# Three instead of two last channel groups taken image by image, with three x tiles loaded one step ahead and three spare buffers for pieces, in a convolution and whitening kernel

## The chip, the core and the metric

The kernel runs on one core of one Trainium2 chip. The metric is the device time of one execution in microseconds (us), the median of several runs. A profile is one execution of the same program, recorded by the hardware profiler; its times are counted from the first recorded instruction. The engines are named as in the profile: PE is the matrix engine (TensorE), PEld its weight loads, DVE the vector engine, ACT the scalar engine, POOL GpSimd, and SP the engine that does nothing here but issue DMAs. Each engine works through its own list of instructions in order.

## The reference: what is computed

The input `x` has 4 images of 64 channels of 256 x 256 float32. Two layers follow each other.

```python
# layer 0: a causal 2-D convolution per channel, with a filter that is an outer product
hx = filter_X(z) * decay          # 256 taps for each of the 64 channels
hy = filter_Y(z) * decay
k  = einsum('ijk,imk->ijmk', hx, hy)
y  = irfft2(rfft2(x) * rfft2(k) / fft_size)[:256, :256] + x * bias
# layer 1: whitening over the 64 channels
x1   = y as (64, 4*256*256)
x1_s = x1[:, ::9]                 # every ninth pixel
cov  = x1_s @ x1_s.T / n + 0.01 * I
out  = isqrt_newton_schulz(cov, 5) @ (x1 - mean(x1_s))
```

Because the 2-D filter is an outer product, layer 0 is two 1-D convolutions, one along each axis of the image, and each of them is a product with a 256 x 256 Toeplitz matrix (each row is the row above, shifted by one tap).

## The kernel before

**Tiling.** The 64 channels are 8 groups of 8 (`CG`). A step is one channel group `g` of one image `n`, so there are 32 steps; `steps` (lines 107 and 108) is their order. The first six groups run group by group, with the four images inside; the last two groups run image by image: (6,0), (7,0), (6,1), (7,1) and so on. The x data of a step is one tile of 128 partitions x 16 KB, of which the pool `xpool` has four. A step has four items of two channels, `c` = 0, 2, 4, 6. This text numbers the items 0 to 127 in their order: item `j` is step `j // 4`, channels `2 * (j % 4)` and the next.

**Matrix work.** An item is multiplied twice by Toeplitz blocks (`f` = 0 in its first stage, `f` = 1 in its second). The function `group` (line 394) computes at once the first stage of one item and the second stage of the item two places before it; this text calls the call for item `j` group `j`. So item `j` has its first stage in group `j` and its second in group `j + 2`. Only the first two items and the last two are computed alone (`half_group`). In a group, 80 recorded matmuls of line 220 alternate between the two items: the first matmul is of the first-stage item, the second of the second-stage item, and so on. Even groups take the four 64-row blocks of the matrix in the order 0, 1, 2, 3 and odd ones in the reverse; in an even group the second matmul reads the upper half (partitions 64 to 127) of the second-stage matrix. After the matmuls ACT copies the first-stage result (line 409), DVE adds bias and x to the second-stage result in place in the x tile (line 412), and `store` (line 420) sends the two channels to `y_d` in DRAM by two DMAs of 256 KB on SP's queue (line 425). `pack` then lets DVE copy sampled pixels to `samp` (line 319), at a pace of some 2.9 us for each group.

**SP's list.** All loads of the loop stand in SP's list, in program order, behind the stores of the same group (lines 587 to 596): first one 512 KB part of x (two channels), then, where the dictionary `blocks` says so, one part of a Toeplitz block (line 193, 192 or 256 KB), then, where the dictionary `early` says so, one 2 MB piece of `y_d` (line 357). As the stores wait for DVE's line 412 of their group, everything of a group's slot in SP's list is issued after that group's matmuls have ended. The DMAs use eight semaphores in turn, and an issue waits until the DMA eight places before it has landed.

**Toeplitz blocks.** `toep[g]` holds both matrices of the 8 channels of a group in 16 KB of each partition; the pool `tpool` has three buffers. A block comes in eight parts: part 0 to 3 is `f` = 0 and 4 to 7 is `f` = 1; in each `f` the first two parts are the lower half of the partitions and the last two the upper half; of each two, the first is channels 0 to 3 and the second channels 4 to 7. The dictionary `blocks` (lines 371 to 376) maps the number of a group to the part that is issued in its slot. In the kernel before, block 6 is issued in the slots of groups 82 to 89 and first used in group 96; block 7 is issued in the slots of groups 90 to 97, its part 6 in that of group 96, and item 100 is the first item of channel group 7, whose second stage is in group 102.

**The end.** When all channels of an image are stored, its 8 pieces of 2 MB can be read back. `homes` names the 13 buffers in which pieces are held, in turn: two of the pool `epool`, three of `tpool`, four of the samples and four of x tiles. Nine pieces are loaded inside the loop (`early`), four more after it, and piece `i + 13` when piece `i` has been written out. `covariance(n)` (line 333, 116 matmuls) takes the samples of one image; it stands on PE in front of a group for images 0 to 2, and after the loop for image 3. `whitening` then makes the 64 x 64 matrix `W` on PE, DVE and ACT, and from there each piece is multiplied by `W` (line 635), evacuated by ACT and DVE (lines 639, 640) and written out (line 645).

Of the kernel before, what the change touches and what calls it, by code (L numbers as in the profile page):

```python
# [38 lines left out]
F32 = mybir.dt.float32  # L39
# [6 lines left out]
NB, C, L = 4, 64, 256  # L46
P, H2 = 128, 2
EMB, ORDER = 33, 64
PIX = L * L
CG = 8  # L50
# [4 lines left out]
EPS = 0.01  # L55
N_ITER = 5
GW = P + L
FP = 4096

TURN = 6.283185  # L60
# [4 lines left out]
def conv_whiten_kernel(ctx: ExitStack, tc: tile.TileContext, a: dict, out: bass.AP):  # L65
    nc = tc.nc
    x = a["x"]

    const = ctx.enter_context(tc.tile_pool(name="const", bufs=1))
    xpool = ctx.enter_context(tc.tile_pool(name="xpool", bufs=4))  # L70
    epool = ctx.enter_context(tc.tile_pool(name="epool", bufs=2))
    spool = ctx.enter_context(tc.tile_pool(name="spool", bufs=NB))
    tpool = ctx.enter_context(tc.tile_pool(name="tpool", bufs=3))
    o1pool = ctx.enter_context(tc.tile_pool(name="o1pool", bufs=4))
# [3 lines left out]
    y_d = [dram.tile([H2 * C, PIX // H2], F32, tag=f"y{n}", name=f"y_d{n}") for n in range(NB)]  # L78
    g_d = dram.tile([P, GW], F32, tag="g", name="g_d")
    g0_d = dram.tile([2 * CG, GW], F32, tag="g0", name="g0_d")  # L80

# [18 lines left out]
    def load_x(t, g, n, c):  # L100
        nc.sync.dma_start(
            out=t[:, c : c + 2],
            in_=x[n, g][:, c : c + 2],
        )


    steps = [(g, n) for g in range(C // CG - 2) for n in range(NB)]
    steps += [(g, n) for n in range(NB) for g in range(C // CG - 2, C // CG)]

    x_tiles = [xpool.tile([P, CG, H2, L], F32, tag="in", name=f"x{u}") for u in range(4)]  # L110
    for c in range(0, CG, 2):
        load_x(x_tiles[0], *steps[0], c)
        if c == 0:
            nc.sync.dma_start(out=decay, in_=a["decay"])
    nc.sync.dma_start(out=mask, in_=a["mask"])
# [5 lines left out]
    for n in range(NB):  # L121
        t = spool.tile([P, FP], F32, tag="samp", name=f"samp{n}")
        samp.append(
# [14 lines left out]

    taps = scratch[:, 11:13, :].rearrange("p a w -> p (a w)")[:, 0:GW]
    nc.gpsimd.memset(taps[:, L:GW], 0.0)  # L140

# [13 lines left out]
    for i in range(3):  # L155
        for u in range(2):
# [3 lines left out]
            arg, k, nxt = (scratch[:, 2 + 3 * i + v, half] for v in range(3))  # L160
# [22 lines left out]
    def new_toeplitz(g):  # L183


        return tpool.tile([P, 2, CG, L], F32, tag="toep", name=f"toep_{g}")

    def load_toeplitz(t, g, f, half, lo=0, hi=CG, issue=nc.sync):
        source, row = (g0_d, f * CG + lo) if g == 0 else (g_d, f * C + g * CG + lo)


        skip = 0 if f == half else HP
        issue.dma_start(
            out=t[half * HP : (half + 1) * HP, f, lo:hi, skip:],
            in_=bass.AP(
                tensor=source.tensor,
                offset=source.offset + row * GW + skip,
                ap=[[1, HP], [GW, hi - lo], [1, L - skip]],
            ),
        )  # L200
# [126 lines left out]
    def covariance(n):  # L327

        pc = psA.tile([P, C + 1], F32, tag="psA", name=f"pc{n}")
        for b in range(H2):  # L330
            for j in range(NJ):
                half = slice(C * (j % 2), C * (j % 2 + 1))
                nc.tensor.matmul(  # L333
                    pc[half],
                    lhsT=samp[n][:, b, j, 0:C],
                    rhs=samp[n][:, b, j, :],
                    start=(b == 0 and j < 2),
                    stop=(b == H2 - 1 and j >= NJ - 2),
                    skip_group_check=True,
                )  # L340
        nc.vector.scalar_tensor_tensor(cov, pc, 1.0 / NSAMP, cov, ALU.mult, ALU.add)


    pieces = [(n, q) for n in range(NB) for q in range(PIX // H2 // FP)]


    homes = [
        {"t": (tpool, "toep"), "s": (spool, "samp"), "i": (xpool, "in"), "e": (epool, "extra")}[k]
        for k in "eetssiistitis"
    ]  # L350

    def load_y(i):

        n, q = pieces[i]
        pool, tag = homes[i % len(homes)]
        t = pool.tile([P, FP], F32, tag=tag, name=f"yi_{n}_{q}")
        nc.sync.dma_start(out=t, in_=y_d[n][:, q * FP : (q + 1) * FP])  # L357
        return t
# [10 lines left out]


    blocks = {}
    for g in range(1, C // CG):
        first = 16 * g - 14 if g < C // CG - 1 else 16 * g - 22
        for part in range(8):
            k = first + (part * 12 // 8 if g < C // CG - 2 else part)
            blocks[k // 4, k % 4 * 2] = (g, part)

    early = {
        (26, 4): 1, (27, 0): 1, (27, 4): 1, (28, 0): 1, (29, 2): 1, (30, 0): 1, (31, 0): 1, (31, 2): 1, (31, 4): 1
    }  # L380
    orders = [list(range(L // HP)), list(reversed(range(L // HP)))]

# [11 lines left out]
    def group(first, second):  # L394

        units = []
        g1, n1, c1, x1, o1s1 = first
        g2, n2, c2, x2, o1s2 = second
        for u in range(2):
            job2 = (bank(f"p2_{g2}_{n2}_{c2 + u}"), o1s2[u], toep[g2][:, 1, c2 + u, :])  # L400
            job1 = (bank(f"p1_{g1}_{n1}_{c1 + u}"), x1[:, c1 + u], toep[g1][:, 0, c1 + u, :])
            units.append((job1, job2))

        toeplitz_products(units, orders[0])
        orders.reverse()
        for u in range(2):
            o1 = o1pool.tile([P, H2, L], F32, tag="o1", name=f"o1_{g1}_{n1}_{c1 + u}")
            for to, fr in ((slice(0, HP), slice(HP, P)), (slice(HP, P), slice(0, HP))):
                nc.scalar.copy(o1[to], units[u][0][0][fr])  # L409
            o1s1.append(o1)  # L410
            ch = g2 * CG + c2 + u
            nc.vector.scalar_tensor_tensor(  # L412
                x2[:, c2 + u], x2[:, c2 + u], bias[:, ch : ch + 1], units[u][1][0],
                ALU.mult, ALU.add,
            )

        store(second)
        pack(2.92)
# [138 lines left out]
    with tc.manual_schedule(  # L557
        engines={engines.PE, engines.SP, engines.DVE, engines.Activation, engines.Pool}
    ):
        toep = {0: new_toeplitz(0)}  # L560

        for f, lo, hi in ((0, 0, 2), (0, 2, 4), (0, 4, 6), (1, 0, 2), (0, 6, 8), (1, 2, 4), (1, 4, 8)):
            for half in range(2):
                load_toeplitz(toep[0], 0, f, half, lo, hi, nc.scalar if half else nc.sync)
        for c in range(0, CG, 2):
            load_x(x_tiles[1], *steps[1], c)
        for i, (g, n) in enumerate(steps):
            xt = x_tiles[i % 4]
            for c in range(0, CG, 2):
                item = (g, n, c, xt, [])  # L570
                if g == C // CG - 1 and n > 0 and c == 2:
                    covariance(n - 1)
                if len(pending) == 2:
                    group(item, pending.pop(0))
                else:
                    half_group(item, 0)
                pending.append(item)
                if i == 0 and c == 6:

                    fold = const.tile([P, C], F32, tag="fold", name="fold")  # L580
                    nc.vector.tensor_tensor(fold, ident[:, 0:C], ident[:, C:P], ALU.add)

                    nc.scalar.activation(bf[:, 0:1], samp[0][:, 0, 0, C : C + 1], AF.Sqrt)
                if i == 1 and c < CG - 2:
                    load_pick(c // 2 * 3, c // 2 * 3 + 3)

                if i + 2 < len(steps):
                    load_x(x_tiles[(i + 2) % 4], *steps[i + 2], c)
                if (i, c) in blocks:
                    tg, part = blocks[i, c]  # L590
                    if part == 0:
                        toep[tg] = new_toeplitz(tg)
                    lo = part % 2 * CG // 2
                    load_toeplitz(toep[tg], tg, part // 4, part // 2 % 2, lo, lo + CG // 2)
                for _ in range(early.get((i, c), 0)):
                    load_next()
        g, n, c, yt, _ = pending[0]
        for item in pending:
            half_group(item, 1)
            pack(1.0)  # L600
            store(item)

        pack()
        i15 = place(2 * C, rows=C).rearrange("p (u c) -> p u c", u=2)
        for u in range(2):
            nc.gpsimd.tensor_scalar(i15[:, u], ident[0:C, 0:C], 1.5, None, ALU.mult)  # L606
        ones = place(P, rows=C)
        nc.gpsimd.memset(ones, 1.0)
        for lo in range(CG // 2, CG, 2):
            pack_by_pe(g, n, yt, slice(lo, lo + 2))  # L610
        spin(4)
        covariance(NB - 1)
        while len(loaded) < len(homes):
            load_next()
        W, shift = whitening(i15, ones)
# [3 lines left out]
    for i, (n, q) in enumerate(pieces):  # L619
# [5 lines left out]
        part = 512 if i == 0 else 1024 if i == 1 or i > len(pieces) - 3 else 2048  # L625
        for w in range(FP // 1024):

# [78 lines left out]
```

## Time and profile before

| What | Value |
|---|---|
| median of 3 runs | 903.03 us (901.62 to 903.9) |
| span of the profiled execution | 902.1 us |
| PE busy | 781.2 us, 87% of the span |
| DVE busy | 581.5 us, 64% |
| ACT busy | 395.5 us, 44% |
| DMA | 285.61 MB, mean 317 GB/s |
| matmuls of line 220 | 10,080 records, 64% of the chain that ended last |
| reads of pieces (line 357) | 32 x 2 MB, median 15.6 us to landing |
| parts of Toeplitz blocks (line 193) | 63 on SP's queue, 3.0 / 5.8 / 7.5 us to landing (least, median, most) |

The profile page has a row of digits for each engine: the span in 40 equal slices of 22.55 us, each digit the busy share of a slice in tenths. PEclk is the granted clock of PE in tenths of full speed. The chain that ended last is followed back from the last instruction, at each step to what released it. An issue of a DMA is shown on SP's queue ("SPq") with the time at which it was issued; "to landing" is the time from there until its semaphore shows the data in place. For about every second DMA the record has no landing of its own.

### The profile page before, as it was taken

To read this page: it belongs to the slowest core of one execution; us is meant where nothing else is said; L and a number is where in the kernel's file an instruction comes from. 1 tells how busy PE (TensorE), PEld (TensorE's weight loads), DVE (VectorE), ACT (ScalarE), POOL (GpSimd) and SP (SyncE) were. 2 spreads that over 40 slices of the span, in tenths; PEclk is the share of its full clock that TensorE was granted. 3 is DMA by queue.
4 is the path that set the end of the run, shared out by engine and by line. 5 is a ranking of instruction groups with operands and counts; after the bars stand their busy time and mean duration, and the time that the engine had idled before them with its cause. 6 is when DMAs were issued, how large, how long until landed. Compare 5 with 4: busy or idle time off the path is not lost.

```text
span 902.1 us, 28046 instructions
## 1 busy us (share of the span) xinstructions
PE 781.2 (87%) x11928; PEld 647.5 (72%) x11928; DVE 581.5 (64%) x801; ACT 395.5 (44%) x676; POOL 14.5 (2%) x40
## 2 busy tenths in 40 slices
PE   8999999999999999999999999999999565666200
PEld 7999999999999999999999999999533111212000
DVE  3487778877888778877888877877688332233200
ACT  2655554545455555545454444442487232233200
POOL 1000000000000000000000000000010000000000
PEclk9999999999999999999999999999999766866755
DMA  7988889798788888888997899979999999999998
GB/s 209 327 262 252 242 261 271 234 273 251 247 263 261 244 264 259 258 250 267 293 275 241 285 351 356 335 237 390 375 401 429 430 432 432 429 434 430 430 430 355
DMA packets 117912, 285.61 MB, mean 317 GB/s; under 512 B 8891, under 2 KB 91116, under 8 KB 110108
## 3 DMA queue, kind: packets, MB, share of 16 engines
q1 hardware_dynamic: 113436, 244.94, 79.0%
q0 software_dynamic: 3056, 37.95, 10.0%
q8 instruction: 95, 1.56, 0.7%
q10 hardware_dynamic: 1296, 0.93, 0.4%
q14 instruction: 29, 0.24, 0.1%
HBM read 149.35 MB, written 134.44 MB: 315 GB/s over the span
## 4 chain that ended last, share of the span: by engine, by line
PE 74%; DMA 11%; another core or an unknown queue 7%; DVE 0%; issue 0%; SPq 0%; ACT 0%; POOLq 0%; DVEq 0%
PE p L220 64%; DMA out_dram<-yi 5%; DMA yi<-y_d 5%; PE po L635 4%; PE pc L333 2%; PE ph L252 1%; PE pk L300 1%; PE spin L442 1%; DMA toep<-g_d 0%; PE busy L152 0%; PE pm L158 0%; SPq L357 0%; DMA scratch<-in_zw_dram 0%; DVE yi L640 0%
## 5 line engine op out<-in xcount | busy, mean ns | idle before, releaser
L220 PE MATMUL p<-toep,x 64*64 64x64 f32 (+3 forms) x5040 | 579.5, 284 | 0.8 <-issue 0.8
L220 PE MATMUL p<-toep,o 64*64 64x64 f32 (+3 forms) x5040 | 579.5, 284 | 0.0
L220 PEld LDWEIGHTS p<-toep,x 64*128 64x128 f32 (+1 forms) x5040 | 535.7, 166 | 24.4 <-issue 1.3
L220 PEld LDWEIGHTS p<-toep,o 64*128 64x128 f32 (+1 forms) x5040 | 536.7, 166 | 10.7 <-issue 0.2
L409 ACT COPY o<-p 64x512 f32<-64x512 f32 x504 | 292.8, 581 | 294.2 <-PE p L220 286.6
L319 DVE COPY_PREDICATED samp<-mask,x 128x464 f32<-128x464 int32 (+3 forms) x351 | 297.2, 847 | 9.8 <-DVE x L412 0.2
L412 DVE SCALAR_TENSOR_TENSOR x<-x,bias,p 128x512 f32<-128x512 f32 x252 | 179.8, 744 | 121.3 <-PE p L220 117.3
L635 PE MATMUL po<-yi,chain 64*64 64x512 f32 x1024 | 143.7, 720 | 60.4 <-DMA yi<-y_d 60.4
L640 DVE TENSOR_SCALAR yi<-po,shift 128x512 f32<-128x512 f32 x128 | 96.1, 751 | 109.0 <-PE po L635 100.7
L635 PEld LDWEIGHTS po<-yi,chain 64*64 64x64 f32 x1024 | 48.0, 162 | 155.2 <-issue 150.5
L639 ACT ACTIVATE yi<-po,shift 128x512 f32<-128x512 f32 x128 | 88.0, 687 | 116.7 <-PE po L635 116.0
L333 PE MATMUL pc<-samp 128*64 128x65 f32 x464 | 14.9, 223 | 0.0
L333 PEld LDWEIGHTS pc<-samp 128*64 128x64 f32 x464 | 14.3, 137 | 0.3
L645 POOL DMA_DIRECT2D out_dram<-yi x19 | 10.5, 554 | 130.5 <-DMA out_dram<-yi 55.1
L606 POOL TENSOR_SCALAR chain<-ident 64x64 f32<-64x64 f32 x2 | 1.0, 519 | 606.6 <-PE ph L252 606.6
L286 DVE COPY o<-ph 64x256 f32<-64x256 f32 x8 | 3.4, 422 | 9.7 <-PE ph L252 9.6
L152 PE MATMUL busy<-idle 128*128 128x128 f32 x64 | 9.4, 307 | 0.0
L152 PEld LDWEIGHTS busy<-idle 128*128 128x128 f32 x64 | 8.9, 222 | 0.2 <-issue 0.2
L300 PE MATMUL pk<-x,pick 128*128 128x56 f32 (+1 forms) x72 | 8.3, 292 | 0.0
L300 PEld LDWEIGHTS pk<-x,pick 128*128 128x128 f32 x72 | 8.1, 192 | 0.1
L442 PE MATMUL spin<-ident 128*128 128x128 f32 x50 | 7.9, 292 | 0.0
L286 ACT COPY o<-ph 64x256 f32<-64x256 f32 x8 | 2.9, 368 | 10.7 <-DMA toep<-g_d 9.2
(93 smaller groups left out, 77.4 us busy)
## 6 DMA issues: line engine op xcount, KB each, us to landing
x<-in_x_dram SPq DMA_DIRECT2D x128, 512.0 KB, 5.3
y_d<-x SPq DMA_DIRECT2D x256, 256.0 KB, 3.5
yi<-y_d SPq DMA_DIRECT2D x32, 2048.0 KB, 15.6
out_dram<-yi POOLq DMA_DIRECT2D x17, 2048.0 KB, 67.7
out_dram<-yi SPq DMA_DIRECT2D x11, 2048.0 KB, 32.9
toep<-g_d SPq DMA_DIRECT2D x28, 256.0 KB, 6.3
toep<-g_d SPq DMA_DIRECT2D x29, 192.0 KB, 5.7
out_dram<-yi SPq DMA_DIRECT2D x4, 1024.0 KB, 32.8
```

The costliest lines, as they stand in the source:

```text
L152: nc.tensor.matmul(p, lhsT=idle[:, 0:P], rhs=idle[:, P : 2 * P], start=True, stop=True)
L220: mm = nc.tensor.matmul(ps[q : q + w, m, HP * k : L], lhsT=src[parts, k // 2, m * P + q : m * P + q + w], rhs=t[parts, : stop : -1] if k e ...
L300: nc.tensor.matmul(pk[:, b, :, 0:nj], lhsT=pick[:, (s - b) % STEP, :], rhs=yt[:, cs, b, s : s + STEP * (nj - 1) + 1 : STEP], start=(s == 0 ...
L319: nc.vector.copy_predicated(dst, m, src)
L333: nc.tensor.matmul(pc[half], lhsT=samp[n][:, b, j, 0:C], rhs=samp[n][:, b, j, :], start=(b == 0 and j < 2), stop=(b == H2 - 1 and j >= NJ ...
L409: nc.scalar.copy(o1[to], units[u][0][0][fr])
L412: nc.vector.scalar_tensor_tensor(x2[:, c2 + u], x2[:, c2 + u], bias[:, ch : ch + 1], units[u][1][0], ALU.mult, ALU.add,)
L442: nc.tensor.matmul(p, lhsT=ident, rhs=ident, start=True, stop=True)
L635: nc.tensor.matmul(po[u][halves[k]], lhsT=W[halves[u]], rhs=v[halves[u], k, cols], start=True, stop=True,)
L639: nc.scalar.activation(v[:, 0, cols], po[0], AF.Identity, bias=shift)
L640: nc.vector.tensor_scalar(v[:, 1, cols], po[1], shift, None, ALU.add)
L645: issue.dma_start(out=o[:, :, end - part : end], in_=v[:, :, end - part : end])
```

## The change

Four things change. The last three channel groups run image by image, (5,0), (6,0), (7,0), (5,1) and so on, instead of the last two. The x tiles are three instead of four, and the x of a step is loaded during the step before it instead of two steps before it; the tiles are used in turn from the second one on, so that the third-last step has the first. `epool` has three buffers instead of two, and `homes` has three of them and three x tiles; there are still 13. The tables of loads are written anew: for each group `g`, `blocks` has the number of the first slot and over how many slots the eight parts are spread, and `early` has nine other places.

```diff
+LATE = 3
-    xpool = ctx.enter_context(tc.tile_pool(name="xpool", bufs=4))
-    epool = ctx.enter_context(tc.tile_pool(name="epool", bufs=2))
+    xpool = ctx.enter_context(tc.tile_pool(name="xpool", bufs=3))
+    epool = ctx.enter_context(tc.tile_pool(name="epool", bufs=3))
...
-    steps = [(g, n) for g in range(C // CG - 2) for n in range(NB)]
-    steps += [(g, n) for n in range(NB) for g in range(C // CG - 2, C // CG)]
-
-    x_tiles = [xpool.tile([P, CG, H2, L], F32, tag="in", name=f"x{u}") for u in range(4)]
+    steps = [(g, n) for g in range(C // CG - LATE) for n in range(NB)]
+    steps += [(g, n) for n in range(NB) for g in range(C // CG - LATE, C // CG)]
+
+    x_tiles = [xpool.tile([P, CG, H2, L], F32, tag="in", name=f"x{u}") for u in range(3)]
+
+    def x_of(i):
+        return x_tiles[(i + 1) % 3]
...
-        for k in "eetssiistitis"
+        for k in "eeessstititis"
...
-    for g in range(1, C // CG):
-        first = 16 * g - 14 if g < C // CG - 1 else 16 * g - 22
+    for g, (first, groups) in {
+        1: (2, 12), 2: (18, 12), 3: (34, 12), 4: (46, 12), 5: (57, 12), 6: (69, 12), 7: (82, 8)
+    }.items():
         for part in range(8):
-            k = first + (part * 12 // 8 if g < C // CG - 2 else part)
-            blocks[k // 4, k % 4 * 2] = (g, part)
+            k = first + part * groups // 8
+            blocks.setdefault((k // 4, k % 4 * 2), []).append((g, part))
 
     early = {
-        (26, 4): 1, (27, 0): 1, (27, 4): 1, (28, 0): 1, (29, 2): 1, (30, 0): 1, (31, 0): 1, (31, 2): 1, (31, 4): 1
+        (23, 4): 1, (24, 0): 1, (24, 4): 1, (25, 0): 1, (27, 6): 1, (30, 4): 1, (30, 6): 1, (31, 2): 1, (31, 4): 1
     }
...
-            xt = x_tiles[i % 4]
+            xt = x_of(i)
             for c in range(0, CG, 2):
                 item = (g, n, c, xt, [])
-                if g == C // CG - 1 and n > 0 and c == 2:
+                if g == C // CG - 2 and n > 0 and c == 2:
                     covariance(n - 1)
...
-                if i + 2 < len(steps):
-                    load_x(x_tiles[(i + 2) % 4], *steps[i + 2], c)
-                if (i, c) in blocks:
-                    tg, part = blocks[i, c]
+                if 0 < i < len(steps) - 1:
+                    load_x(x_of(i + 1), *steps[i + 1], c)
+                for tg, part in blocks.get((i, c), ()):
```

The line `halves = g >= C // CG - 2` in `store`, which splits the sampling of the last groups in two, is not touched.

More of the change, by code (lines that the diff above doesn't have):

```diff
@@ L104, in load_x @@
         )
-    steps = [(g, n) for g in range(C // CG - 2) for n in range(NB)]
-    steps += [(g, n) for n in range(NB) for g in range(C // CG - 2, C // CG)]
-    x_tiles = [xpool.tile([P, CG, H2, L], F32, tag="in", name=f"x{u}") for u in range(4)]
+    steps = [(g, n) for g in range(C // CG - LATE) for n in range(NB)]
[3 more added lines that the diff above has]
+        return x_tiles[(i + 1) % 3]
     for c in range(0, CG, 2):
-        load_x(x_tiles[0], *steps[0], c)
+        load_x(x_of(0), *steps[0], c)
         if c == 0:
@@ L565, in conv_whiten_kernel @@
         for c in range(0, CG, 2):
-            load_x(x_tiles[1], *steps[1], c)
+            load_x(x_of(1), *steps[1], c)
         for i, (g, n) in enumerate(steps):
-            xt = x_tiles[i % 4]
+            xt = x_of(i)
             for c in range(0, CG, 2):
                 item = (g, n, c, xt, [])
-                if g == C // CG - 1 and n > 0 and c == 2:
+                if g == C // CG - 2 and n > 0 and c == 2:
                     covariance(n - 1)
```

## The prediction

> **What bounds the kernel now.** I read the page's slices first, then the chain that ended last in order of time, then the busy time by stretches.
>
> ```profile
> PE   8999999999999999999999999999999565666200
> DMA  7988889798788888888997899979999999999998
> ...
> 22.51 60.85 PE p L220 x1072
> 83.73 430.31 PE p L220 x7458
> ...
> 613.60 5.79 PE ph L252 x57
> ...
> 643.25 27.70 PE po L635 x256
> ```
>
> PE is full until about slice 31, and DMA is full from slice 27 on. The chain lies on the loop's matmuls (line 220) from 22.5 to 613.6 us, with three covariances among them, then on PE's work after the loop; at 643.25 `W` is ready and line 635 begins. So the loop is bound by PE. By stretches (length, then busy us of PE, PEld, DVE, ACT, POOL, then granted clock, DMA share and GB/s):
>
> ```profile
> 400.00:500.00 100.00, 100.00 (x1756) 94.09 (x1755) 81.18 (x106) 50.35 (x87) 0.00 (x0) 1.00 0.88 267
> 590.00:600.00 10.00, 10.00 (x235) 9.41 (x234) 8.88 (x16) 4.65 (x8) 0.00 (x0) 1.00 0.39 128
> 614.00:643.00 29.00, 27.83 (x329) 25.45 (x325) 17.12 (x52) 3.58 (x17) 1.15 (x3) 1.00 1.02 416
> 643.00:645.50 2.50, 2.50 (x27) 1.00 (x29) 1.02 (x2) 1.24 (x3) 0.00 (x0) 1.00 0.72 301
> 645.50:650.00 4.50, 4.50 (x48) 1.57 (x44) 3.96 (x6) 3.65 (x6) 0.00 (x0) 1.00 0.75 278
> 700.00:847.00 147.00, 86.94 (x504) 27.95 (x496) 47.00 (x63) 43.06 (x63) 3.74 (x7) 0.72 1.01 430
> ```
>
> In the loop PE has no idle time at all. After 650 the DMA engines are the bound, at 430 GB/s. Between the two bounds, at 643 to 650, the DMA share falls to about 0.75: the 13 pieces that have a home were all read as `W` became ready, and nothing more could move before the first output. So the last stretch is fixed bytes counted from `W`: 32 outputs and 32 - 13 = 19 reads, 51 x 2.097 MB = 107 MB, 249 us at 430 GB/s; from 645.6 that is 894.5, and the span is 902.1, with smaller descriptors at both ends. Whatever delays PE in the loop delays `W`, and so the end, one for one; whatever only moves DMA work within the loop gains nothing.
>
> **The change, part by part.**
>
> *Pieces, homes, order of images: 0 us.* Nine pieces are still read in the loop and four after it, into 13 homes, so the 107 MB stay. The three covariances are only moved (3.64 us each in the chain, in both). What earlier reading can gain is the DMA idle time around `W`: 2.5 x 0.28 + 4.5 x 0.25 = 1.8 us. I take 0, since these outputs wait for `W` and not for DMA; bounds -1.8 and 0. The matmuls, copies and stores are the same in number.
>
> *Block 7: the term that matters.* In group-by-group order there was time for the last blocks. Now channel group 7 first comes at step 22, group 88, and its second stage at group 90. Only three buffers exist and blocks 5, 6 and 7 fill them, so block 7 must wait until block 4 is done (group 81), and it stands in the slots of groups 82 to 89. Its part 6 (second matrix, upper half, channels 0 to 3) goes out in the slot of group 88. Group 90 is even: its second matmul multiplies item 88 by that upper half. Before, the shortest way of any part from slot to use was six groups; now it is two. In the kernel before, block 6 stands in the very same slots, with the same two stores and one x load ahead of each part, so its record gives the times. SP's issues around group 88's slot, and PE at the start of group 90 (start, length):
>
> ```profile
> 423.71 0.88 SPq L425 DMA_DIRECT2D y_d<-x  x2
> 424.69 1.43 SPq L101 DMA_DIRECT2D x<-in_x_dram  x1
> 426.17 0.58 SPq L193 DMA_DIRECT2D toep<-g_d  x1
> 427.92 0.88 SPq L425 DMA_DIRECT2D y_d<-x  x2
> ...
> 426.69 0.38 PE L220 MATMUL p<-toep,x 64*128 64x256 f32 x1
> 426.69 0.38 PE L220 MATMUL p<-toep,o 64*128 64x256 f32 x1
> ```
>
> The block loads from 397.64 on are parts 0, 1, 2 and so on; the one at 426.17 is part 6. Group 90's second matmul stands at 426.69, half a microsecond later. Time to landing (least, median, most) of the line 193 loads from 397 to 450, then of the x loads in that stretch, then of the x loads from 505 to 590:
>
> ```profile
> DMA to landing us min/median/max: 5.3/5.9/7.1
> ...
> DMA to landing us min/median/max: 4.9/5.9/6.5
> ...
> DMA to landing us min/median/max: 4.3/6.1/10.0
> ```
>
> Part 6 lands at 426.17 + 5.3 to 7.1 = 431.5 to 433.3, so PE stands for 4.8 to 6.6 us; with the 3.0 us that is the least of all line 193 loads it would be 2.5. I take 5.0, near the lower row, because the x load ahead of it took 1.43 us to issue and the queue had drained meanwhile. Nothing covers it: PE takes its list in order, groups 91 and on stand behind, and PE had no idle time to give back. ACT (line 409), DVE (line 412) and the stores of group 90 are late by the same. Part 7 (slot of 89, issued at 429.37, landed by 436.5 with 7.1) is used from group 92 on, which then begins no earlier than 440: no second wait. Blocks 1 to 6 keep at least seven groups each: 0.
>
> [...]
>
> *PE's clock after the stall: 2.0 us.* The loop runs at a granted clock of 1.00. In the last stretch PE waits for pieces, and the clock falls:
>
> ```profile
> 708.39 5.36 PE L635 MATMUL po<-yi,chain 64*64 64x512 f32 x32 [6.06 <-DMA yi<-y_d]
> 718.11 5.36 PE L635 MATMUL po<-yi,chain 64*64 64x512 f32 x32 [4.36 <-DMA yi<-y_d]
> ...
> 715.30:718.70 3.40, 0.59 (x8) 0.38 (x12) 0.00 (x0) 0.00 (x0) 0.00 (x0) 1.00 0.97 414
> 718.70:722.10 3.40, 3.40 (x24) 1.28 (x19) 1.49 (x2) 1.38 (x2) 0.22 (x1) 0.50 1.03 439
> ```
>
> After 4.36 us of idling PE ran the next 3.4 us at 0.50, though busy all the while. Line 220's pairs follow each other every 0.21 us and stream all that time, so half a clock should lose half the time: 1.7 us for one such stretch, 3.4 for two. I take 2.0; bounds 0 and 3.4.
>
> [...] The row shows the drop after a gap that left PE 0.59 us of work in the window, so I keep it likely.
>
> *x one step ahead: 0 us.* The x load in the slot of group u is now needed by group u + 4. With the slot of group 88 (x at 424.69), and group 92 beginning 2 x 4.61 = 9.2 us after 426.69 (one group: 430.31 us / 93.2 groups of 80), that leaves 11.2 us. The loads take 4.9 to 6.5 in the plain loop. Where 2 MB pieces stand in front, up to 10.0 is recorded, leaving 1.2. The new table puts the first four pieces two groups apart with the covariance in between, just as the old one did, so I cost it 0; bounds 0 and 2, because not every landing is recorded. If pieces bunch, x is late next, and PE with it. At the start, step 2's x is issued one step later; that only thins a queue from which PE, already 60.5 us busy in 60.5 us, did not wait.
>
> **Sum.** 902.1 + 5.0 + 2.0 = 909.1 us for a profile. The median of the runs stands 0.9 us above the profiled span, so 910.0.
>
> **The rivals.**
>
> *The wait never shows (903.5).* If part 6 came early enough, for instance because SP's slot moved ahead of group 89's end, 0 to 1 us remain. Against: the stores ahead of it wait for DVE's line 412 of group 88, which cannot end before that group's matmuls.
>
> *x loads become the bound (918).* With pieces in front, three or four x loads miss their group by 2 to 3 us each: 910 + 8. For: 1.2 us of reserve beside a 10.0 us row, and four pieces in the slots of groups 122 to 126, beside x loads until 123. Against: the order is the old one, and old rows would have fitted.
>
> *Early reads win (899).* The DMA queue is empty of reads when `W` comes, so outputs run at once at 430 GB/s: 1.8 us of idle share, and 650 to 665, where 372 GB/s moved, would gain 15 x 58 / 430 = 2.0: 903.0 - 3.8. It decides only if the stall at group 90 is below these 3.8 us. Against: in 650 to 665 the DMA share is 1.02 already, so small descriptors and not a lack of work hold it.
>
> **How the numbers follow.** Chances: forecast 0.73, x bound 0.12, no wait 0.09, early reads 0.06. The forecast's own bounds are 903.0 + 2.5 + 0 = 905.5 and 903.0 + 6.6 + 3.4 + 2 = 915.0. That alone leaves out 0.27, so the range goes down to 903.2 and takes in the wait that never shows; 0.18 is left out, early reads and the x bound. About 0.3% (2.7 us) is what a measurement can tell from no change: faster 0.06; same 0.09, the wait that never shows; slower 0.85.
>
> **What would show it.** In the new profile PE idles once for some 5 us near 427, at line 220's counterpart, released by a load of the last block; the clock is 0.50 for 3.4 or 6.8 us right after; `W` and the first output come some 7 us later than 643.25 and 645.57; from there to the end it is again some 256 us. A full PE across 427, or several idle spots released by x loads, makes the prediction wrong; so does a first output at the old time with an earlier end.

## The result, and the profile after

The changed kernel takes 912.06 us (median of 4 runs, 911.3 to 913.82) against 902.98 us for the kernel before: a ratio of 1.0107, 95% interval 1.0092 to 1.0122, so about 9.1 us slower. A second set of runs gave 1.0119 (1.0105 to 1.0133). The profiled span went from 902.1 to 911.7 us; the profile of the changed kernel is of the longest of its four runs (913.82 us).

The page of the changed kernel, PE, its granted clock and DMA in 40 slices (now of 22.8 us):

```profile
PE   8999999999999999998999999999999466566300
PEclk9999999999999999998999999999999876776855
DMA  7788788788889888888589859779999999999998
```

One slice of the loop, the 19th (410 to 433 us), is no longer full, and the clock falls in that slice too. The chain that ended last says where (start, length, what):

```profile
22.39 398.70 PE p L225 x6922
...
423.43 1.43 SPq L102
424.90 5.27 DMA toep<-g_d
430.31 34.56 PE p L225 x552
464.87 3.64 PE pc L338 x116
468.51 0.49 PE p L225 x19
469.00 2.13 issue
471.12 56.64 PE p L225 x936
...
622.24 5.79 PE ph L257 x57
...
651.89 22.79 PE po L640 x209
```

(Line 225 is line 220 of the kernel before, 338 is 333, 418 is 412, 640 is 635, 198 is 193.) In the kernel before, the chain stayed on PE without a break from 83.73 to 514.05. Now it leaves PE twice. At 424.90 it runs through the load of a Toeplitz part, 5.27 us from issue to landing; at 469.00 there are 2.13 us in which PE waits for nothing that the profile shows. The waits inside the loop (us in total, times, longest) name the same two spots:

```profile
PE p L225 <- DMA toep<-g_d: 4.0, 1, 4.0
PE p L225 <- issue: 2.1, 1, 2.1
```

PE itself around the first spot, group 90 (start, length):

```profile
425.47 0.38 PE L225 MATMUL p<-toep,o 64*128 64x256 f32 x1
425.68 0.59 PE L225 MATMUL p<-toep,x 64*128 64x256 f32 x2
430.31 0.76 PE L225 MATMUL p<-toep,o 64*128 64x256 f32 x1 [4.04 <-DMA toep<-g_d]
430.32 0.79 PE L225 MATMUL p<-toep,x 64*128 64x256 f32 x1
430.87 0.63 PE L225 MATMUL p<-toep,o 64*128 64x256 f32 x1
430.90 0.63 PE L225 MATMUL p<-toep,x 64*128 64x256 f32 x1
431.29 0.63 PE L225 MATMUL p<-toep,o 64*128 64x256 f32 x1
```

The first matmul of the group, of the first-stage item (`x`), runs at 425.68; the first of the second-stage item (`o`) waits until 430.31. After the wait the pairs follow each other every 0.43 us instead of every 0.21. By stretches (PE, PEld, DVE, ACT, POOL, then clock, DMA share, GB/s):

```profile
427.00:432.00 5.00, 1.69 (x8) 1.56 (x10) 2.28 (x4) 0.48 (x1) 0.00 (x0) 0.61 0.99 299
432.00:436.00 4.00, 4.00 (x32) 3.84 (x31) 0.00 (x0) 0.00 (x0) 0.00 (x0) 0.64 0.24 44
436.00:440.00 4.00, 4.00 (x108) 3.81 (x107) 2.76 (x5) 2.32 (x4) 0.00 (x0) 1.00 0.15 47
```

From 432 to 436 PE is busy all the time and does 32 matmuls at 0.64 of the clock; from 436 on it runs at 1.00. DMA stands nearly idle after 432, at a share of 0.24 and then 0.15: SP's next stores, those of group 90, go out at 438.60.

Where the 9.6 us of the two spans went, worked out from the starts of the groups in the records (us; group 16 to 88 is 72 groups, 88 to 91 is three, 91 to 126 holds all three covariances of the loop):

| Kernel | start to 16 | 16 to 88 | 88 to 91 | 91 to 126 | 126 to line 635 | from there to the end |
|---|---|---|---|---|---|---|
| before | 87.46 | 330.29 | 13.68 | 172.86 | 38.89 | 258.96 |
| changed | 86.55 | 330.00 | 20.63 | 175.75 | 38.90 | 259.88 |
| difference | -0.91 | -0.29 | +6.95 | +2.89 | 0.0 | +0.92 |

### The profile page after: what moved, and what is told of

The parts are those of the page before. It is cut to its first block, busy times and chain, and to the rows that moved or that the text cites. A ratio compares the mean times of both kernels' runs of the same rounds, so it can differ in the third digit from the quotient of the medians.

```text
span 911.7 us, 28015 instructions
## 1 busy us (share of the span) xinstructions
PE 782.1 (86%) x11928; PEld 649.6 (71%) x11928; DVE 580.6 (64%) x801; ACT 395.1 (43%) x676; POOL 14.5 (2%) x40
## 3 DMA queue, kind: packets, MB, share of 16 engines
q1 hardware_dynamic: 113436, 244.94, 77.5%
q8 instruction: 94, 1.54, 0.7%
## 4 chain that ended last, share of the span: by engine, by line
PE 72%; DMA 11%; another core or an unknown queue 8%; issue 1%; DVE 1%; SPq 1%; ACT 0%; DVEq 0%; POOLq 0%
PE p L225 63%; DMA yi<-y_d 5%; DMA out_dram<-yi 5%; PE po L640 3%; PE pc L338 2%; PE ph L257 1%; DMA toep<-g_d 1%; PE pk L305 1%; PE spin L448 1%; PE busy L157 0%; PE pm L163 0%; SPq L362 0%; DMA scratch<-in_zw_dram 0%; DVE yi L645 0%
## 5 line engine op out<-in xcount | busy, mean ns | idle before, releaser
L640 PE MATMUL po<-yi,chain 64*64 64x512 f32 x1024 | 141.3, 710 | 63.8 <-DMA yi<-y_d 63.8
L346 DVE SCALAR_TENSOR_TENSOR cov<-pc,cov 128x65 f32<-128x65 f32 x4 | 0.9, 227 | 11.5 <-PE pc L338 11.5
```

The lines of the kernel that those rows point to most:

```text
L640: nc.tensor.matmul(po[u][halves[k]], lhsT=W[halves[u]], rhs=v[halves[u], k, cols], start=True, stop=True,)
```

## The experiments

Each ratio is to the kernel before, run beside it on the same chip, with its 95% interval.

**Block 7 earlier.** All its parts go out in the slots of groups 82 to 85.

```diff
-        ... 7: (82, 8)
+        ... 7: (82, 4)
```

> All eight parts of block 7 are issued in the slots of groups 82 to 85, two in each, instead of one in each of 82 to 89; nothing else differs from the changed kernel. Theory (the wait for part 6 of block 7 at group 90 and the halved clock behind it cost 7.0 us, from the profiles: groups 88 to 91 took that much longer than before): the idle spot near 426 us and the halved clock after it are gone, the other idle spot after the first covariance stays, and the time is 912.1 - 7.0 = 905.1. Rival (the DMA queue is the limit, so the wait only moves to x loads): another idle spot at groups 86 to 92 and 909 or more.

Measured: 906.4 us, 1.0044 (1.0024 to 1.0065). Groups 88 to 91 take 13.86 us (13.68 before the change), with no idle spot; the second spot stays (chain of this kernel):

```profile
458.04 3.64 PE pc L338 x116
461.68 0.49 PE p L225 x18
462.17 2.14 issue
464.31 56.51 PE p L225 x938
```

So the wait did not move elsewhere. The spot that is left comes after the same number of matmuls behind the covariance, 18 or 19, though everything stands 7 us earlier.

**The wait filled with work.** The changed kernel, with matmuls of the identity that nothing reads.

```diff
+                if (i, c) == (22, 4):
+                    spin(18)
                 if len(pending) == 2:
```

> The changed kernel with 18 matmuls of 128x128 of the identity put on PE in front of group 90, which fill most of the wait for part 6 with work that nothing reads. Theory (the wait itself is 4.6 us and the clock that falls to half behind it costs another 2.3 us): the wait stays, the clock stays at 1.00 across it, and the time is 912.1 - 2.3 = 909.8. Rival (the clock costs nothing, line 225's stream is bound by something else, or the clock falls anyway): 912 or more.

Measured: 911.73 us, 1.0106 (1.0088 to 1.0124): the forecast of 909.8 failed, though in the profile the clock stayed at 1.00 and groups 88 to 91 took 18.23 us, 2.4 less than in the changed kernel (this profile is of a run of 910.82 us, that of the changed kernel of one of 913.82). The other spot did not go; it moved, and this told more than the filling itself:

```profile
426.18 4.21 PE spin L448 x36
430.39 32.40 PE p L225 x558
462.79 3.12 PE pc L338 x99
465.91 2.20 issue
468.11 0.69 PE pc L338 x17
```

The filling is 36 recorded matmuls. The idle spot stood after 116 + 19 = 135 matmuls from the covariance's start, and stands now after 99: exactly 36 fewer. It belongs to a place in PE's list of instructions and not to any tile. The records of DMA packets have a queue for instructions (q8, of kind "instruction" on the page: 94 packets, 1.54 MB in the changed kernel) with packets of 16 KB, one every 7.2 us on average between 100 and 400 us. Around the covariance:

```
kernel                         packet before   next packet starts   PE resumes   idle
changed                            457.25           468.69            471.12      2.13
changed, again                     456.89           468.43            470.80      2.04
block 7 earlier                    450.38           462.00            464.31      2.14
block 7 earlier, again             450.20           461.31            463.65      1.95
wait filled                        454.88           465.83            468.11      2.20
kernel before (at its covariance)  512.86           518.88            521.17      0.47
pieces after the covariance        457.05           465.23              -         none
```

Where PE idled, it resumed 2.3 to 2.4 us after the start of a packet, each time. Both together point to PE having run out of instructions, and a count of the records of PE and PEld (matmuls, weight loads and their semaphore instructions) from the start of the list agrees. Ahead of the 0.37 us at 83 us in the kernel before stand 2,498 records, and 9 packets had started; ahead of its 0.47 us at 521 us, 18,113 and 70. Between the two lie 15,615 records and 61 packets, 256 records to a packet. The 2.13 us at the covariance here fit in: 16,066 records and 62 packets. Each of the three stands behind 256 records for each packet and 193 or 194 more. The wait for part 6, which has a releaser, does not fit this count: 14,659 records and 57 packets, 67 more.

**Pieces after the covariance.** The changed kernel, with its first four pieces three groups later.

```diff
-        (23, 4): 1, (24, 0): 1, (24, 4): 1, (25, 0): 1, ...
+        (24, 2): 1, (24, 6): 1, (25, 2): 1, (25, 6): 1, ...
```

> The changed kernel with its first four pieces of y three groups later, in the slots of groups 97, 99, 101 and 103 instead of 94, 96, 98 and 100, so that none is issued ahead of the first covariance. Theory (the second idle spot, 2.1 us at 469 us with half a clock behind it, is PE's instruction fetch, queued behind a 2 MB piece while the covariance's short matmuls use up instructions twice as fast): no idle spot there, group 97 takes its usual 4.6 us, and the time is 912.1 - 4.2 = 907.9; the wait at group 90 stays. Rival (it is an x load or a PSUM bank that is late after the covariance): an idle spot of like size in groups 97 to 104 and 911 or more.

Measured: 909.88 us, 1.0084 (1.0069 to 1.0099). The spot is gone, and nothing like it stands in groups 97 to 104:

```profile
464.40 3.64 PE pc L338 x116
468.04 27.41 PE p L225 x464
```

The time fell by 2.1 us against the 4.2 forecast. From group 91 to 126 the profile has 172.26 us, 3.5 less than the changed kernel. The spot and the clock after it were sized well: group 97 takes 4.65 us here and 8.77 in the changed kernel. But some 0.7 us are lost anew around the start of group 108, at a wait that the expectation did not have: with the pieces later an x load took 11.65 us to land, and PE stood 0.35 us for it (the line after it is group 108).

```profile
507.09 11.65 DMA x<-in_x_dram
518.88 4.90 PE p L225 x78
```

The rest, 3.5 us against 2.1, is within the intervals of the runs.

**x one step ahead, alone,** in the kernel before: three x tiles, a third buffer in `epool`, the order of steps, blocks and early loads as before.

```diff
-        for k in "eetssiistitis"
+        for k in "eetsseistitis"
...
-                if i + 2 < len(steps):
-                    load_x(x_tiles[(i + 2) % 4], *steps[i + 2], c)
+                if 0 < i < len(steps) - 1:
+                    load_x(x_of(i + 1), *steps[i + 1], c)
```

> The kernel before with the x part of the change alone: three x tiles loaded one step ahead, a third buffer in epool, and a home of that buffer in place of the third x tile (sixth in turn); two last groups image by image, blocks and early loads as before. Theory (x one step ahead has a reserve of 1.2 us or more and costs nothing): 902 to 904, the same as before. Rival (x loads become late behind pieces): 905 or more, with idle spots of PE released by x loads between 505 and 590 us.

Measured: 902.54 us, 1.0004 (0.9995 to 1.0014). No PE wait on an x load. This part and the third buffer cost nothing and bring nothing.

**Both idle spots out:** block 7 in 82 to 85, pieces three groups later.

> The changed kernel with both edits: block 7 two parts to a slot (groups 82 to 85), and the first four pieces three groups later (97, 99, 101, 103). Theory (two idle spots of PE and the clock behind them are all that the change costs; the rest of it is worth nothing because the last stretch is bound by DMA): PE has no idle spot over 1 us in the loop, W is ready at about 641.5, and the time is that of the kernel before, 901.5 to 904. Rival (the new order itself costs something in the loop or at its end): 905 or more.

Measured: 903.48 us, 1.0001 (0.9992 to 1.0010). PE is full around both places (stretches of this kernel):

```profile
425.00:435.00 10.00, 10.00 (x172) 9.37 (x170) 8.88 (x16) 4.72 (x9) 0.00 (x0) 1.00 0.75 239
455.00:480.00 25.00, 25.00 (x479) 23.59 (x475) 17.04 (x23) 9.88 (x18) 0.00 (x0) 1.00 0.75 251
```

The whole loss is given back by these two edits, and nothing of a gain is left over. (Two spots remained. The 0.98 us at 83 us are shown as "issue", behind the same 1,072 matmuls of the loop as the 0.37 us of the kernel before. The 0.52 us at 513 us are a wait for DVE's line 418, in front of group 108, where the kernel with the pieces alone moved waits for x.)

**The clock once more,** with the pieces after the covariance, meant to keep the second spot out: the same 18 matmuls in front of group 90.

> The kernel with the pieces three groups later (909.9, block 7 as in the change), with 18 matmuls of 128x128 in front of group 90 that nothing reads, which fill the wait for part 6. It repeats the test of the clock without the idle spot at the covariance, which moved in the first one. Theory (the half clock behind the wait costs 1.7 to 2.3 us): the clock stays at 1.00 and the time is 907.9. Rival (it costs well under 1 us on the average run): 909.5 or more.

Measured: 909.19 us, 1.0067 (1.0055 to 1.0079), beside 1.0084 without the filling: 1.5 us less, with intervals of 1.1 to 1.4 us on either side of each. In the profile the clock stays at 1.00 and PE is full:

```profile
426.00:436.00 10.00, 9.96 (x150) 9.28 (x150) 3.96 (x8) 1.99 (x5) 0.00 (x0) 1.00 0.65 188
```

Groups 88 to 91 take 18.79 us against 20.38, so in the profiles the filling saves 1.6 to 2.4 us there. But the second spot did disturb: with the covariance 36 matmuls later in PE's list, 0.81 us of it came back though no piece stands ahead of the covariance, and 0.52 us stood at the third covariance.

```profile
462.90 3.12 PE pc L338 x99
466.02 0.81 issue
466.83 0.69 PE pc L338 x17
```

Groups 91 to 126 take 173.99 us against 172.26, and the two profiled spans are equal (907.7 us). So these two kernels do not settle what the clock costs the average run.

**The covariance in halves.** The changed kernel, with 58 of a covariance's matmuls in front of each of two groups (the edit inside `covariance` that takes the halves is not shown).

```diff
-                if g == C // CG - 2 and n > 0 and c == 2:
-                    covariance(n - 1)
+                if g == C // CG - 2 and n > 0 and c in (2, 4):
+                    covariance(n - 1, [c // 2 - 1])
```

> The changed kernel with each of the three covariances of the loop in two halves of 58 matmuls, in front of two groups instead of one; pieces and block 7 as in the change. Theory (PE uses up its instructions faster in a covariance than the fetch behind a 2 MB piece brings them): half the burst between two fetches leaves an idle spot under 1 us near 469 and 908 to 910. Rival (the fetch is late by itself, whatever PE's pace): the idle spot stays near 2 us and the time 911 to 913.

Measured: 912.16 us, 1.0103 (1.0090 to 1.0116). The idle spot is gone from the profile (the only one left after group 91 is 0.3 us long, at 499), but the time did not follow within its interval. Groups 91 to 126 took 173.82 us, 1.9 less than in the changed kernel, not the 3.1 to 3.5 that moving the pieces brought. As the two disagreed, the same was tried where block 7 is not late, three kernels side by side on one chip.

> Block 7 two parts to a slot and each covariance of the loop in two halves; pieces as in the change. It asks whether the halves, which took the idle spot out of the profile but left the time at 912.2, are worth their idle spot where the wait for block 7 is gone. Theory (the idle spot at the covariance costs 2 to 4 us, and halves remove most of it): 902.5 to 904.5. Rival (its instructions are late anyway, in smaller portions): as with block 7 alone, 906 or more.

> The changed kernel as it is, on the same chip as the two beside it, for a comparison without other chips between. Theory: 911.5 to 912.5.

> Block 7 two parts to a slot, as before, for the same comparison. Theory (7.0 us in the profile for the wait and the clock behind it): 905 to 906.5, 5.5 to 7 us under the change beside it. Rival (the clock costs nothing on the average run): 4.6 us under it, 907.5.

Measured: 903.68 us, 1.0012 (1.0003 to 1.0021) with both; 913.4 us, 1.0119 (1.0105 to 1.0133) for the change; 906.33 us, 1.0040 (1.0027 to 1.0053) for block 7 alone. So block 7's wait is worth 7.1 us, with some 1.7 us on either side by the two intervals: the rival, a clock that costs the average run nothing, had 4.6 and lies outside. The halves are worth 2.65 us (2.8 us between groups 91 and 126 of the two profiles). The change itself measured above its forecast band.

**The last pieces earlier as well,** in the kernel with both edits.

```diff
-        ... (30, 4): 1, (30, 6): 1, (31, 2): 1, (31, 4): 1
+        ... (30, 2): 1, (30, 4): 1, (31, 0): 1, (31, 2): 1
```

> As the kernel with both edits, and the sixth to ninth piece one or two groups earlier, as soon as their homes are free (groups 121, 122, 124, 125 instead of 122, 123, 125, 126). Theory (in the changed order the reads before W end some microseconds after W is ready, so that DMA sets the end): the reads end earlier and the time is 900.5 to 902, at or just under the kernel before. Rival (the end is set by W alone, or x loads behind the pieces become late): the same as the kernel with both edits, or slower.

Measured: 904.28 us, 1.0017 (1.0009 to 1.0025). A miss: no gain, and a little slower than the kernel before. From line 635 to the end it took 259.5 us, where the other kernels run for the experiments have 259.5 to 260.1, whatever their loops did. So `W` sets the end, and reading earlier does not. No version tried is faster than the kernel before.

## Why the prediction was right, and where it was short

*The bound.* Right. Delays of PE in the loop reached the end one for one (`W` later by 8.64 us in the profile, 643.25 to 651.89, the span by 9.6), and the earlier reading of pieces gained nothing: with both spots out the time is the old one.

*Block 7.* Right in place, cause and size. Part 6, issued in the slot of group 88 at 424.90, was waited for by the second matmul of group 90; it took 5.27 us to land where the rows gave 5.3 as the least. The stall was 4.6 us (425.68 to 430.31) for the 5.0 taken.

*The clock.* Right in the profile: 2.3 us (4.6 us at half), for the 2.0 taken; together 6.95 of the forecast 7.0, so close only because 0.4 too much for the wait and 0.3 too little for the clock cancel. In the profiles before and after the change, every stretch of one granted clock in the trace's clock records but the last is a multiple of 3.413 us long. The changed kernel has half clock for 6.83 us from 428.08, at the wait, and for 3.41 us from 472.46, behind the spot at the covariance. Cut into such lengths of 3.413 us from the start of the clock records on, the two profiles show the clock fall from full 32 times, each time after a length with 1.81 us or more of PE idle, and hold after 417, none with more than 2.00 us (by the records, in which the ends of matmuls are modelled). The length ahead of the fall at the covariance has 2.1 us idle. In the four profiles with a spot of about 2 us there and no filling, the 936 to 940 matmuls up to the second covariance took 56.5 to 56.6 us; with the wait filled, 958 took 55.04 us, the pace of the stretch up to the third (960 in 55.18), so half clock did not cost anything there.

*x one step ahead.* Right: 0 in the changed kernel. The reserve of 1.2 us was as thin as it looked: with the first pieces later, one x load was late by 0.35 us.

*The covariances: the step that was short.* The prediction costed them at nothing because they "are only moved". They cost 2.9 us (group 91 to 126): group 97 takes 4.1 us longer, for an instruction packet that came late (the spot of 2.13 us) and 3.41 us of half clock behind the spot, while the covariance used 116 matmuls in 3.64 us, almost twice the pace of the loop's 80 in 4.6; and 1.1 us less are lost in groups 109 to 111, where the kernel before has its own first covariance. The row was there to be read, in the chain before:

```profile
514.05 3.64 PE pc L333 x116
517.69 3.01 PE p L220 x63
520.70 0.47 issue
```

The section on x even noted that "the covariance in between" was the same as in the old table, and took that for cover. It is the same: a piece is issued 6.4 us before the covariance's start and another 2.8 us after it in the kernel before, 5.6 and 2.9 us in the changed one. What differs is the place at which PE runs out, 135 matmuls behind the covariance's start instead of 179, and the interval between the packets, 11.4 us instead of 6.0. Why the packet came so much later is not in the trace.

*Start and end.* Costed at 0 and 0; the profiles differ by -1.2 us up to group 88 and by +0.9 after line 635. The first is mostly the 0.7 us that group 15 of the kernel before loses around 83 us, its 0.37 us of "issue" among them; the kernel with both edits, which also loads x one step ahead, lost 1.3 us there (87.72 us to group 16), so it is scatter and not the change. The second rests on the one profile of the kernel before: x one step ahead alone has 259.96 us there and the time of the kernel before. It stays open.

## What to carry to other kernels

When a buffer ring is one short, look for the load that is issued last and used first: its slot, the slot of its first use and one row of landing time give the stall before anything is run, and sending the load's parts two at a time where the buffer is already free took it out here. A gap of 2 to 5 us in PE's work cost here the time of the gap and up to 2.3 us of clock behind it. An idle spot with no releaser that stayed at the same count of PE's instructions when work was put in front of it pointed to the fetch of instructions here: count the records from the start of the list. Moving the 2 MB reads away from the burst of short matmuls, or halving the burst, took the 2 us out; small spots remained either way (0.35 us in front of group 108, 0.3 us at 499).

## What the runs showed of the hardware that was not expected

The page counts the instruction packets of queue q8 on the same 16 DMA engines as the data (0.7% of the engines' span in the changed kernel, beside 77.5% for q1), and here some came late. At the covariance the interval between two of them was 10.9 to 11.6 us in the five profiles with an idle spot of about 2 us, 9.9 us in the one with 0.81 us, and 8.0 to 8.5 us in the three with the pieces moved and nothing filled in, where PE did not idle. With the covariance in halves it was again 11.3 and 11.5 us, without an idle spot, and in the loop of the changed kernel 11.5 us from 321 us on and 12.0 us from 542 us on, also without one: in these profiles a late packet cost 2 us only at the covariance's 116 matmuls in 3.64 us. In the plain loop the longest such spot is 0.98 us.

The records also show how much slack there was. In the loops of the profiles before and after the change, the packet that starts earliest by PE's count, number 22 of the changed kernel at 170.47 us, starts when PE has done 83 records less than 256 times its number, and at the three idle spots counted above PE stands at 193 or 194 more than 256 times the packets started until then. An estimate from that: a packet that starts as early leaves PE 277 records, which is 7.9 us of work at the loop's 35 records per us (3,511 in the 100 us from 400 to 500 in the kernel before) and 4.3 us at the covariance's 64 (232 in 3.64 us), and at the covariance 2.3 to 2.4 us pass from a packet's start until PE resumes, by the table above. When the fetch was asked for is not in the trace, so how long it queued was not measured.
